# Latent attention's layer norms on ScalarE and GpSimd, its keys masked by GpSimd, and a beginning of one tile

## The chip, the cores and the metric

The kernel runs on one core of a Trainium2 chip. The metric is the device time of one execution in microseconds (us); less is better. Five engines work beside each other, each through its own queue of instructions in order: TensorE (PE, matmuls; its weight loads are PEld), VectorE (DVE), ScalarE (ACT), GpSimd (POOL) and SyncE (SP, which here only issues DMA transfers). SBUF is the memory that the engines work in, PSUM the one that matmuls write to.

## The reference

Four layers run over a tensor x of 32 x 256 tokens with 128 features, fp32. Each layer has an attention-like half and an MLP-like half, and each half works on a modulated layer norm:

```
mod = (silu(c) @ wmod).reshape(32, 6, 1, 128)       # sa, ca, ga, sb, cb, gb; gates held at 0.25 or more
h = layernorm(x) * (1 + ca) + sa;  x = x + ga * attn(h)
h = layernorm(x) * (1 + cb) + sb;  x = x + gb * ffn(h)
```

Layer 3's attention is the latent attention: 16 heads of 8 features, no mask, keys and values from a latent of 32 features.

```
q = h @ Wq + bq;  latent = h @ Wl + bl
k = latent @ Wk + bk;  v = latent @ Wv + bv
out = softmax(q k^T / sqrt(8)) v, per sequence of 256 tokens and per head;  out @ Wo + bo
```

Its MLP quantizes its input and weights to a 4-bit grid in blocks of 16 (fp4) before three matmuls with a SiLU gate. Layer 0's first half is a selective scan.

## The kernel before, in words

The 8192 tokens are 16 tiles (NB) of 512 tokens (TB), each kept in SBUF as x[b], 128 features by 512 tokens. The program goes through eight stages, two per layer: scan_layer, dense_moe, hale, capacity_moe, phase_attention, head_moe, latent_attention, fp4_mlp.

**Order.** A stage writes its work into an agenda of numbered slots (put(t, ...)) and then issues it slot by slot. mm (L386) and tr (L390), all matmuls and transposes, are always kept in that written order; VectorE's instructions too while `nc.vector.on` (L298 is the wrapper through which they go, so that most of VectorE's rows carry L298); ScalarE's only while `strict_act` is set, which it is in scan_layer and fp4_mlp and not in latent_attention. Where nothing is kept, a scheduler places the instruction in its engine's queue. The queue that results is fixed, and an engine that waits holds up all behind it.

**Beginning.** begin (L602 to L634) loads c and wmod of all four layers in one transfer, mw, computes the modulation of each layer (six matmuls, and copies into self.mods), and loads the 16 x tiles (xin; even ones through ScalarE's queue, odd ones through SP's), turns each by four transposes and copies it (by VectorE or ScalarE in turn) into x[b]. Only then the pools of scan_layer (L637) open. Its agenda begins at slot -44 of tile 0: norm_rows, scan_roots, norm_scale, norm_out and so on, a chain that reaches the first scan (hs, L849) at slot 0.

**Latent attention** (L2449). attention() gives a tile 16 slots, eight for each of two sequences. In each slot come first the score matmuls for the row maxima ("max", S<-kx,q; VectorE reduces them to mt), then those for the exponentials ("exp", S<-qa,kx; ScalarE writes E), then the rest: the values (po<-E,vz, two slots after their E), and the work on other tiles. Two sets of scores per slot share three PSUM buffers of S; one further buffer, tp, serves transposes and small matmuls, and one, po, the values. The queries qa carry the negated maximum in a ninth row of each head, taken in by a transpose of mt (tp<-cst,mt) at two slots per sequence.

The work before tile b is spread over the tile ahead of it: 14 slots ahead the norm's rows (head), 13 and 12 ahead its two parts, 10 ahead back (norm_out), 8 latent, 6 q, 4 keys, 2 v. Its output projection and residual come at slot 4 two tiles later, and from 3 slots after that the tile's MLP norm and quantization (mlp_front through mlp_ahead, tag fx and qx): mlp_norm at slot 7, its parts at 8 and 9, mlp_h at 11, mlp_rows at 15. The last tile's MLP norm lies in fp4_mlp. During tiles 7 to 9 the MLP's weights are quantized too.

**A norm** (two per tile): norm_rows (L440) turns x by four transposes into tp, ScalarE copies them to SBUF (ln_xn, or fx for the MLP), VectorE takes statistics (bn_stats, bn_aggr) and v = variance + eps (ln_v). norm_place (L456) then computes 1/sqrt(v) by an integer first guess and Newton steps on 128x4 values, all on VectorE (newton_parts, L934: 2 integer and 12 small operations in two parts), and scales the rows in place: four instructions of 128x128. norm_out turns the rows back (tp<-cst,ln_xn, or tp<-cst,fx).

**Keys** (keys, L1528): two matmuls put both halves of the 16 heads into S (128x1024). Four ScalarE activations (L1536) write kx: each 128x512 with a scale of one or zero per partition (c.half, which keeps one of two neighbouring heads) and a bias (key_bias, L133), which also writes the ones of the ninth row.

Of the kernel before, what the change touches and what calls it, by code (L numbers as in the profile page):

```python
# [25 lines left out]
ALU = mybir.AluOpType  # L26
# [115 lines left out]

def rows(v):

    v = np.asarray(v, np.float32).reshape(1, -1)
    return np.broadcast_to(v, (P, v.shape[1]))
# [29 lines left out]
def packs(d):  # L176
# [8 lines left out]
    k.add("cT", np.stack([np.asarray(d[f"L{n}_c"]).T for n in range(4)], 1))  # L185
    k.add("wmod", np.stack([np.asarray(d[f"L{n}_wmod"]) for n in range(4)], 1))
# [83 lines left out]
    k.add("Wk", spread(g["Wk"]))  # L270
# [3 lines left out]
    k.add("kb", key_bias(g["bk"]))  # L274
# [35 lines left out]
class Program:  # L310
# [162 lines left out]
    def norm_newton(self, mv, v, r):  # L473


        pool = self.nc.gpsimd
        t = self.wk("ln_t", (P, 4))
        pool.tensor_tensor(t, r, r, ALU.mult)
        pool.tensor_tensor(t, t, v, ALU.mult)
        pool.tensor_scalar(t, t, -0.5, 1.5, ALU.mult, ALU.add)  # L480
        pool.tensor_tensor(r, r, t, ALU.mult)
        shift = self.wk("ln_m", (P, 4))
        pool.tensor_tensor(shift, mv[:, :, 0], r, ALU.mult)
        pool.tensor_scalar(shift, shift, -1.0, None, ALU.mult)
        return r, shift

# [115 lines left out]
    def begin(self):  # L602
        nc, tc = self.nc, self.tc
        nc.scalar.preload_act_table_set(LN_EXP)
        with ExitStack() as ctx:
            self.pools(ctx, {"tp": 4, "mod": 2}, xin=3, mw=1)
            mw = self.wk("mw", (P, self.at["mod"]["n"]))
            nc.scalar.dma_start(mw, self.aps["mod"])
            v = View(mw, self.at["mod"]["at"])
            for n in range(4):  # L610
                sg = self.wk("sg", (P, NSEQ))
                self.sigmoid(sg, v.cT[:, n, :])
                nc.vector.tensor_tensor(sg, sg, v.cT[:, n, :], ALU.mult)
                ps = self.ps("mod", (P, 6, NSEQ))
                for j in range(6):
                    nc.tensor.matmul(ps[:, j, :], v.wmod[:, n, j * P : (j + 1) * P], sg, start=True, stop=True)
                m = self.mods[:, n]
                for j in (0, 3):
                    nc.scalar.copy(m[:, j, :], ps[:, j, :])
                    nc.vector.tensor_scalar(m[:, j + 1, :], ps[:, j + 1, :], 1.0, None, ALU.add)  # L620
                    neg, mag = self.wk("neg", (P, NSEQ)), self.wk("mag", (P, NSEQ))
                    nc.vector.tensor_scalar(neg, ps[:, j + 2, :], -1.0, None, ALU.mult)
                    nc.vector.tensor_tensor(mag, ps[:, j + 2, :], neg, ALU.max)
                    nc.vector.tensor_scalar(mag, mag, 0.25, 2.0, ALU.max, ALU.mult)
                    nc.vector.tensor_scalar(neg, ps[:, j + 2, :], 0.0, 0.5, ALU.is_ge, ALU.subtract)
                    nc.vector.tensor_tensor(m[:, j + 2, :], neg, mag, ALU.mult)
            xd = self.aps["x"].rearrange("(b t p) f -> b p t f", p=P, t=4)
            for b in range(NB):
                xi = self.wk("xin", (P, 4, P))
                (nc.sync if b % 2 else nc.scalar).dma_start(xi, xd[b])  # L630
                ps = self.ps("tp", (P, 4, P))
                for t in range(4):
                    nc.tensor.transpose(ps[:, t, :], xi[:, t, :], self.c.ident)
                (nc.scalar.copy if b % 2 else nc.vector.tensor_copy)(self.x[b], ps.rearrange("p a b -> p (a b)"))  # L634


    def scan_layer(self, w):  # L637
# [7 lines left out]
        with ExitStack() as ctx:  # L645
            self.pools(
                ctx, {"dB": 1, "hT": 1, "y": 1, "tp": 1},
                h=4, z=3, dl=3, duT=3, bc=3, xn=1, ln_xn=1, xp=1, y=1, yT=1, rows=1, Xc=1, du=1, sg=1, hsT0=1, hsT1=1, sp_m=1, sp_r=1, Xr=1,
# [21 lines left out]

            for p in range(-1, 8 * NB + 3):
                put(2 * p, self.scan_even, s, p)
                put(2 * p + 1, self.scan_odd, s, p)
# [854 lines left out]
    def keys(self, h, w, bias):  # L1528

        k4 = self.wk("kx", (P, 2, 2, TB))  # L1530
        pk = self.ps("S", (P, 2, TB))
        for x in (0, 1):
            self.mm(pk[:, x, :], w[:, x, :], h)
        for x in (0, 1):
            for j in (0, 1):
                self.nc.scalar.activation(  # L1536
                    k4[:, x, j, :],
                    pk[:, x, :],
                    AF.Identity,
                    bias=bias[:, x, j : j + 1],  # L1540
                    scale=self.c.half[:, j : j + 1],
                )
        return k4
# [905 lines left out]
    def latent_attention(self, w):  # L2449
        nc, c = self.nc, self.c  # L2450
        self.mlp_start()
        with ExitStack() as ctx:
# [7 lines left out]
            def before(b, tiles):  # L2460
                t = tiles[b] = {"vz": self.vzs[4 * (b % 2) : 4 * (b % 2) + 4]}

                def head():
                    t["st"] = self.norm_rows(self.x[b])
                    t["norm"] = self.norm_place(*t["st"])
# [17 lines left out]
                def k():  # L2483
                    t["k4"] = self.keys(t["lat"][:32, :], w.Wk, w.kb)
# [101 lines left out]
    def mlp_norm(self, a):  # L2586
        a["st"] = self.norm_rows(self.x[a["b"]], tag="fx")
        a["norm"] = self.norm_place(*a["st"])
# [211 lines left out]
```

## Time and profile before

| | us |
|---|---|
| three timed runs | 6774.54, 6795.66, 6796.21 (median 6795.66) |
| the profiled execution, whole | 6771.9 |
| its span in the profile | 6769.9 |
| beginning, until TensorE's first transposes for a norm | 44.8 |
| latent stage, tiles 2 to 14 (5784.4 to 6446.9) | 662.5 |
| last stage (6560 to 6770) | 210, VectorE 194 of it busy |

Granted clock of TensorE over the span: 0.918. How to read the lines that follow: a row of the profile names line, engine, operation and tile, output<-inputs, then the shape and count. Times are microseconds, and in rows of groups the mean is in nanoseconds. In brackets stands how long the engine was idle before it and which instruction ended that (<-). A row of a stretch gives from:to, length, and the busy time of each engine with its count of instructions. In rows of waits stand total, times and longest.

### The profile page before, as it was taken

Reading aid. Unit: us, or ns where it says so; the run is one execution under the profiler, and the core shown is the slowest. Engines: PE = TensorE matmul, PEld = TensorE weight load, DVE = VectorE, ACT = ScalarE, POOL = GpSimd, SP = SyncE. Lnnn points to the kernel's source line nnn. Section 1 sums busy time; section 2 is a strip of 40 time slices with the busy share of each in tenths; the row PEclk is TensorE's granted clock in tenths of the full one; section 3 lists DMA queues with packets and bytes.
Section 4 is the critical chain, followed back from the end, with each engine's and each line's share of the span. In section 5 each row is a group of like instructions: output and inputs, shape, how many; then the busy total and the mean of one; then the engine's idle time right before and its main releaser. Section 6 shows DMA issues by size and latency. Waiting matters only on the chain. (4 is left out here: it accounts for less than half of the span.)

```text
span 6769.9 us, 132928 instructions
## 1 busy us (share of the span) xinstructions
PE 5927.9 (88%) x54369; PEld 3341.0 (49%) x54369; DVE 4278.6 (63%) x9929; ACT 3493.9 (52%) x5035; POOL 2650.5 (39%) x2882
## 2 busy tenths in 40 slices
PE   5888886999899999999999767999889998999987
PEld 3555554466455555555566434555422222444444
DVE  3777776611455555555565644777777775677779
ACT  4888884333344444444444322443468886545542
POOL 3555553565444444444444443434234543000000
PEclk6999997999899999999999877888989998999998
DMA  1110111144000000000000101111134442000010
GB/s 60 41 41 29 41 41 35 42 124 119 15 6 5 5 8 5 5 8 5 5 2 2 47 17 26 26 24 26 31 79 90 92 91 49 16 18 18 18 33 30
DMA packets 175445, 232.19 MB, mean 34 GB/s; under 512 B 46519, under 2 KB 95919, under 8 KB 174450
## 3 DMA queue, kind: packets, MB, share of 16 engines
q1 hardware_dynamic: 120656, 124.40, 7.2%
q0 software_dynamic: 26992, 56.62, 3.5%
q10 hardware_dynamic: 27186, 42.67, 1.7%
q8 instruction: 426, 6.98, 0.4%
q14 instruction: 185, 1.52, 0.1%
HBM read 88.22 MB, written 74.97 MB: 24 GB/s over the span
## 5 line engine op out<-in xcount | busy, mean ns | idle before, releaser
L1418 ACT ACTIVATE E<-S 128x1024 f32<-128x1024 f32 x448 | 458.6, 1024 | 602.6 <-PE S L386 535.5
L298 DVE TENSOR_REDUCE mt<-S 128x4 f32<-128x1024 f32 (+1 forms) x512 | 549.8, 1087 | 252.5 <-PE S L386 196.1
L849 DVE TENSOR_TENSOR_SCAN hs<-decay,dB 128x512 f32<-128x512 f32 x512 | 583.0, 1204 | 91.8 <-PE dB L386 77.2
L386 PE MATMUL S<-qa,kx 32*128 32x256 f32 x4096 | 566.8, 396 | 59.8 <-DVE mt L298 39.0
L393 ACT ACTIVATE hid<-S,bigw 128x1024 f32<-128x1024 f32 x512 | 537.2, 1111 | 122.6 <-PE S L386 121.9
L1887 DVE TENSOR_TENSOR E<-S,cst 128x1024 f32<-128x1024 f32 x320 | 391.2, 1223 | 307.3 <-PE S L386 270.7
L1890 POOL TENSOR_SCALAR_AFFINE_SELECT E<-E 128x1024 f32<-128x1024 f32 x320 | 349.3, 1092 | 588.2 <-ACT E L1889 587.9
L386 PE MATMUL S<-kx,q 32*128 32x512 f32 (+1 forms) x2048 | 549.1, 631 | 16.9 <-ACT kx L1536 16.1
L1889 ACT COPY E<-S 128x1024 f32<-128x1024 f32 x320 | 323.5, 1011 | 328.4 <-PE S L386 244.7
L2439 POOL TENSOR_TENSOR acc<-acc,ye 128x512 f32<-128x512 f32 x256 | 344.5, 1346 | 362.7 <-DVE ye L298 319.6
L386 PEld LDWEIGHTS S<-qa,kx 32*128 32x128 f32 x4096 | 360.2, 200 | 178.4 <-DVE mt L298 107.1
L1719 DVE TENSOR_REDUCE mt<-S 128x4 f32<-128x512 f32 (+1 forms) x256 | 205.2, 823 | 320.9 <-PE S L386 312.4
L386 PE MATMUL S<-qG,f 32*128 32x512 f32 x2560 | 382.6, 658 | 4.5 <-DVE E L1887 3.4
L386 PE MATMUL S<-hm,bigw 32*128 32x512 f32 x2048 | 337.3, 650 | 24.8 <-ACT hid L393 24.8
L393 ACT ACTIVATE hsT<-hT 128x1024 f32<-128x1024 f32 x256 | 260.7, 1018 | 157.3 <-PE hT L390 156.2
L393 ACT ACTIVATE decay<-dl,A 128x510 f32<-128x510 f32 x512 | 339.1, 714 | 0.0
L386 PE MATMUL po<-E,vzl 128*32 128x128 f32 x8192 | 286.8, 281 | 59.6 <-POOL E L1890 59.3
L390 PE MATMUL hT<-cst,hs 128*128 128x128 f32 x2048 | 295.9, 290 | 22.6 <-ACT hsT L393 21.4
L386 PE MATMUL po<-hid,bigw 128*32 128x512 f32 x2048 | 279.9, 619 | 31.0 <-DVE ye L298 31.0
L386 PE MATMUL po<-E,vz 128*32 128x256 f32 x4096 | 304.7, 383 | 0.3 <-ACT oc L1438 0.2
L1422 POOL TENSOR_SCALAR_AFFINE_SELECT E<-E 128x512 f32<-128x512 f32 (+1 forms) x192 | 157.7, 822 | 364.4 <-ACT E L1418 363.9
L1766 ACT ACTIVATE E<-S 128x768 f32<-128x768 f32 (+1 forms) x192 | 168.9, 880 | 239.4 <-PE S L386 239.4
(524 smaller groups left out, 13192.1 us busy)
## 6 DMA issues: line engine op xcount, KB each, us to landing
gb<-gT SPq DMA_DIRECT2D x256, 256.0 KB
regions<-zeros ACTq DMA_DIRECT2D x16, 2048.0 KB
rx<-far SPq DMA_DIRECT2D x64, 256.0 KB
expert_rows<-eo SPq DMA_DIRECT2D x39, 256.0 KB
out<-out SPq DMA_DIRECT2D x16, 256.0 KB
xTd<-xT SPq DMA_DIRECT2D x15, 256.0 KB
xT<-xTd SPq DMA_DIRECT2D x15, 256.0 KB
bigw<-in_s SPq DMA_DIRECT2D x10, 256.0 KB
```

The lines of the kernel that those rows point to most:

```text
L298: return lambda *args, **kw: self.tc.keep_in_program_order(op(*args, **kw))
L386: return self.tc.keep_in_program_order(self.nc.tensor.matmul(out, lhsT, rhs, start=start, stop=stop, **kw))
L390: return self.tc.keep_in_program_order(self.nc.tensor.transpose(out, in_, self.c.ident[:k, :k]))
L393: ins = self.nc.scalar.activation(*args, **kw)
L849: nc.vector.tensor_tensor_scan(hs[:, :, n], decay, dB[:, :, n], 0.0, ALU.mult, ALU.add)
L1418: nc.scalar.activation(e, src, AF.Exp, scale=scale)
L1719: nc.vector.tensor_reduce(m.rearrange("p (g j) -> p g j", j=2), pm[:, :, x] if i == 0 else pm[:, :, :, 0:192], AX.X, ALU.max, negate=True,)
L1766: nc.scalar.activation(e, src, AF.Exp, scale=1.0 / math.sqrt(8))
L1887: nc.vector.tensor_tensor(e, src, self.c.caus.unsqueeze(1).to_broadcast([P, 8, P]), ALU.mult)
L1889: nc.scalar.copy(e, src)
L1890: nc.gpsimd.affine_select(e, e, [[0, 8], [1, P]], ALU.is_ge, 0.0, base=0, channel_multiplier=-1)
L2439: nc.gpsimd.tensor_tensor(a["acc"], a["acc"], ye, ALU.add)
```

## The change

Three edits. No work outside the beginning, latent attention and the MLP norms of fp4_mlp is edited.

1. *Beginning.* mod and x are brought in piece by piece. With the scan stage in the program, begin handles layer 0's modulation and x[0] alone; the other 15 tiles (load_in, turn_in) and three layers (mod_load, mod_layer) are put into scan_layer's agenda, at slots -45 to -15 (loads two slots before each turn) and -44 to -22. All x loads go through SP's queue, all x copies are VectorE's; loads of mod stay on ScalarE's queue.
2. *Norms of layer 3.* norm_apart takes norm_place's place: ln_v by GpSimd, Ln and Exp by ScalarE (norm_roots), one Newton step and the four scalings by GpSimd.
3. *Keys.* masked_keys: the bias is a 33rd row of the weights (key_row), against the row of ones that lat already has; one ScalarE copy of 128x1024 to SBUF (kk); two GpSimd multiplications by c.half, 128x1024 each, write kx.

```diff
--- before.py
+++ after.py
@@ -140,6 +140,13 @@
     return out.reshape(4, P).T.reshape(P, 2, 2)
 
 
+def key_row(b):
+
+    full = spread(np.asarray(b)[None]).reshape(1, 2, 8, 16)
+    full[:, :, :, 8] = 1.0
+    return full.reshape(1, 2, P)
+
+
 def rows(v):
 
     v = np.asarray(v, np.float32).reshape(1, -1)
@@ -182,8 +189,7 @@
         return g
 
     k = Pack()
-    k.add("cT", np.stack([np.asarray(d[f"L{n}_c"]).T for n in range(4)], 1))
-    k.add("wmod", np.stack([np.asarray(d[f"L{n}_wmod"]) for n in range(4)], 1))
+    k.add("mod", np.stack([np.concatenate([np.asarray(d[f"L{n}_c"]).T, np.asarray(d[f"L{n}_wmod"])], 1) for n in range(4)], 1))
     out["mod"] = k
 
     g, k = layer(0, "attn"), Pack()
@@ -267,11 +273,10 @@
     g, k = layer(3, "attn"), Pack()
     k.add("Wq", spread(g["Wq"]))
     k.add("Wl", g["Wl"])
-    k.add("Wk", spread(g["Wk"]))
+    k.add("Wk", np.concatenate([spread(g["Wk"]), key_row(g["bk"])], 0))
     k.add("Wo", gathered(g["Wo"]))
     k.add("Wv", np.concatenate([g["Wv"], g["bv"][None]], 0))
     k.add("bq", spread(g["bq"][None])[0].T)
-    k.add("kb", key_bias(g["bk"]))
     k.add("bo", col(g["bo"]))
     k.add("bl", g["bl"][:, None])
     out["s6"] = k
@@ -470,7 +475,7 @@
         self.act(r, t, AF.Exp, scale=-0.5)
         return r
 
-    def norm_newton(self, mv, v, r):
+    def norm_newton(self, mv, v, r, shifted=True):
 
 
         pool = self.nc.gpsimd
@@ -479,10 +484,23 @@
         pool.tensor_tensor(t, t, v, ALU.mult)
         pool.tensor_scalar(t, t, -0.5, 1.5, ALU.mult, ALU.add)
         pool.tensor_tensor(r, r, t, ALU.mult)
+        if not shifted:
+            return r, None
         shift = self.wk("ln_m", (P, 4))
         pool.tensor_tensor(shift, mv[:, :, 0], r, ALU.mult)
         pool.tensor_scalar(shift, shift, -1.0, None, ALU.mult)
         return r, shift
+
+    def norm_apart(self, xn, mv, v):
+
+        r = self.norm_roots(v)
+        yield
+        r, _ = self.norm_newton(mv, v, r, False)
+        for n in range(4):
+            self.nc.gpsimd.tensor_scalar(
+                xn[:, n, :], xn[:, n, :], mv[:, n, 0:1], r[:, n : n + 1], ALU.subtract, ALU.mult
+            )
+        yield
 
     def norm_scale(self, xn, r, shift):
         for n in range(4):
@@ -600,38 +618,51 @@
 
 
     def begin(self):
-        nc, tc = self.nc, self.tc
-        nc.scalar.preload_act_table_set(LN_EXP)
+
+        self.nc.scalar.preload_act_table_set(LN_EXP)
+        some = 0 in self.stages
         with ExitStack() as ctx:
-            self.pools(ctx, {"tp": 4, "mod": 2}, xin=3, mw=1)
-            mw = self.wk("mw", (P, self.at["mod"]["n"]))
-            nc.scalar.dma_start(mw, self.aps["mod"])
-            v = View(mw, self.at["mod"]["at"])
-            for n in range(4):
-                sg = self.wk("sg", (P, NSEQ))
-                self.sigmoid(sg, v.cT[:, n, :])
-                nc.vector.tensor_tensor(sg, sg, v.cT[:, n, :], ALU.mult)
-                ps = self.ps("mod", (P, 6, NSEQ))
-                for j in range(6):
-                    nc.tensor.matmul(ps[:, j, :], v.wmod[:, n, j * P : (j + 1) * P], sg, start=True, stop=True)
-                m = self.mods[:, n]
-                for j in (0, 3):
-                    nc.scalar.copy(m[:, j, :], ps[:, j, :])
-                    nc.vector.tensor_scalar(m[:, j + 1, :], ps[:, j + 1, :], 1.0, None, ALU.add)
-                    neg, mag = self.wk("neg", (P, NSEQ)), self.wk("mag", (P, NSEQ))
-                    nc.vector.tensor_scalar(neg, ps[:, j + 2, :], -1.0, None, ALU.mult)
-                    nc.vector.tensor_tensor(mag, ps[:, j + 2, :], neg, ALU.max)
-                    nc.vector.tensor_scalar(mag, mag, 0.25, 2.0, ALU.max, ALU.mult)
-                    nc.vector.tensor_scalar(neg, ps[:, j + 2, :], 0.0, 0.5, ALU.is_ge, ALU.subtract)
-                    nc.vector.tensor_tensor(m[:, j + 2, :], neg, mag, ALU.mult)
-            xd = self.aps["x"].rearrange("(b t p) f -> b p t f", p=P, t=4)
-            for b in range(NB):
-                xi = self.wk("xin", (P, 4, P))
-                (nc.sync if b % 2 else nc.scalar).dma_start(xi, xd[b])
-                ps = self.ps("tp", (P, 4, P))
-                for t in range(4):
-                    nc.tensor.transpose(ps[:, t, :], xi[:, t, :], self.c.ident)
-                (nc.scalar.copy if b % 2 else nc.vector.tensor_copy)(self.x[b], ps.rearrange("p a b -> p (a b)"))
+            self.pools(ctx, {"tp": 4, "mod": 2}, xin=3, mw=2)
+            for n in (0,) if some else range(4):
+                self.mod_layer(n, self.mod_load(n), self.ps("mod", (P, 6, NSEQ)))
+            for b in (0,) if some else range(NB):
+                self.turn_in(b, self.load_in(b), self.ps("tp", (P, 4, P)))
+
+    def mod_load(self, n):
+
+        mw = self.wk("mw", (P, NSEQ + 6 * P))
+        self.nc.scalar.dma_start(mw, self.aps["mod"][:, n * (NSEQ + 6 * P) : (n + 1) * (NSEQ + 6 * P)])
+        return mw
+
+    def mod_layer(self, n, mw, ps):
+
+        nc = self.nc
+        sg = self.wk("msg", (P, NSEQ))
+        self.sigmoid(sg, mw[:, :NSEQ])
+        nc.vector.tensor_tensor(sg, sg, mw[:, :NSEQ], ALU.mult)
+        for j in range(6):
+            self.mm(ps[:, j, :], mw[:, NSEQ + j * P : NSEQ + (j + 1) * P], sg)
+        m = self.mods[:, n]
+        for j in (0, 3):
+            nc.scalar.copy(m[:, j, :], ps[:, j, :])
+            nc.vector.tensor_scalar(m[:, j + 1, :], ps[:, j + 1, :], 1.0, None, ALU.add)
+            neg, mag = self.wk("neg", (P, NSEQ)), self.wk("mag", (P, NSEQ))
+            nc.vector.tensor_scalar(neg, ps[:, j + 2, :], -1.0, None, ALU.mult)
+            nc.vector.tensor_tensor(mag, ps[:, j + 2, :], neg, ALU.max)
+            nc.vector.tensor_scalar(mag, mag, 0.25, 2.0, ALU.max, ALU.mult)
+            nc.vector.tensor_scalar(neg, ps[:, j + 2, :], 0.0, 0.5, ALU.is_ge, ALU.subtract)
+            nc.vector.tensor_tensor(m[:, j + 2, :], neg, mag, ALU.mult)
+
+    def load_in(self, b):
+        xi = self.wk("xin", (P, 4, P))
+        self.nc.sync.dma_start(xi, self.aps["x"].rearrange("(b t p) f -> b p t f", p=P, t=4)[b])
+        return xi
+
+    def turn_in(self, b, xi, ps):
+
+        for t in range(4):
+            self.tr(ps[:, t, :], xi[:, t, :])
+        self.nc.vector.tensor_copy(self.x[b], ps.rearrange("p a b -> p (a b)"))
 
 
     def scan_layer(self, w):
@@ -645,7 +676,7 @@
         with ExitStack() as ctx:
             self.pools(
                 ctx, {"dB": 1, "hT": 1, "y": 1, "tp": 1},
-                h=4, z=3, dl=3, duT=3, bc=3, xn=1, ln_xn=1, xp=1, y=1, yT=1, rows=1, Xc=1, du=1, sg=1, hsT0=1, hsT1=1, sp_m=1, sp_r=1, Xr=1,
+                h=4, z=3, dl=3, duT=3, bc=3, xn=1, ln_xn=1, xp=1, y=1, yT=1, rows=1, Xc=1, du=1, sg=1, hsT0=1, hsT1=1, sp_m=1, sp_r=1, Xr=1, mw=1,
             )
             self.strict = self.strict_act = True
             wk = self.wk
@@ -668,6 +699,13 @@
             def put(t, f, *args):
                 agenda.setdefault(t, []).append((f, args))
 
+
+            for b in range(1, NB):
+                put(2 * b - 47, lambda b=b: s.update({("xi", b): self.load_in(b)}))
+                put(2 * b - 45, lambda b=b: self.turn_in(b, s["xi", b], self.ps("dB", (P, 4, P))))
+            for n in (1, 2, 3):
+                put(8 * n - 52, lambda n=n: s.update({("mw", n): self.mod_load(n)}))
+                put(8 * n - 46, lambda n=n: self.mod_layer(n, s["mw", n], self.ps("y", (P, 6, NSEQ))))
             for p in range(-1, 8 * NB + 3):
                 put(2 * p, self.scan_even, s, p)
                 put(2 * p + 1, self.scan_odd, s, p)
@@ -1542,6 +1580,23 @@
                 )
         return k4
 
+    def masked_keys(self, lat, w):
+
+        pk = self.ps("S", (P, 2, TB))
+        for x in (0, 1):
+            self.mm(pk[:, x, :], w[:, x, :], lat)
+        both = self.wk("kk", (P, 2, TB))
+        self.nc.scalar.copy(both, pk)
+        k4 = self.wk("kx", (P, 2, 2, TB))
+        for x in (0, 1):
+            self.nc.gpsimd.tensor_tensor(
+                k4[:, x],
+                both[:, x, :].unsqueeze(1).to_broadcast([P, 2, TB]),
+                self.c.half.unsqueeze(2).to_broadcast([P, 2, TB]),
+                ALU.mult,
+            )
+        return k4
+
 
     def hale(self, w):
         nc, c = self.nc, self.c
@@ -2461,8 +2516,8 @@
                 t = tiles[b] = {"vz": self.vzs[4 * (b % 2) : 4 * (b % 2) + 4]}
 
                 def head():
-                    t["st"] = self.norm_rows(self.x[b])
-                    t["norm"] = self.norm_place(*t["st"])
+                    t["st"] = self.norm_rows(self.x[b], nc.gpsimd)
+                    t["norm"] = self.norm_apart(*t["st"])
 
                 def part():
                     next(t["norm"])
@@ -2481,7 +2536,7 @@
                     t["q"] = self.query(t["h"], w.Wq, w.bq)
 
                 def k():
-                    t["k4"] = self.keys(t["lat"][:32, :], w.Wk, w.kb)
+                    t["k4"] = self.masked_keys(t["lat"], w.Wk)
 
                 def v():
                     pv = ps("tp", (P, 4, P))
@@ -2584,8 +2639,8 @@
         yield
 
     def mlp_norm(self, a):
-        a["st"] = self.norm_rows(self.x[a["b"]], tag="fx")
-        a["norm"] = self.norm_place(*a["st"])
+        a["st"] = self.norm_rows(self.x[a["b"]], self.nc.gpsimd, "fx")
+        a["norm"] = self.norm_apart(*a["st"])
 
     def mlp_h(self, a):
         a["h"] = self.norm_out(a["st"][0], self.ada_mods(3, 1, a["b"]), "fh")
```

## Prediction

> **What bounds the kernel now.** I read the page, then the busy times by stretch, TensorE's waits and the order of time in one tile. Busy columns are us of PE, PEld, DVE, ACT, POOL; then granted clock, DMA share, GB/s. The rows are tiles 2 to 14 of the latent stage, and tile 4 alone:
>
> ```profile
> PE 5927.9 (88%) x54369; PEld 3341.0 (49%) x54369; DVE 4278.6 (63%) x9929; ACT 3493.9 (52%) x5035; POOL 2650.5 (39%) x2882
> ...
> 5784.40:6446.90 662.50, 613.81 (x4879) 311.91 (x4879) 495.19 (x1247) 341.60 (x433) 5.68 (x11) 0.94 0.06 17
> 5883.50:5931.60 48.10, 44.61 (x376) 22.73 (x374) 37.35 (x95) 26.11 (x34) 0.52 (x1) 1.00 0.06 19
> ```
>
> TensorE bounds the stage: 44.61 of 48.10 us busy in tile 4, GpSimd idle. An average tile takes 662.5/13 = 50.96 us, 2.86 more than tile 4, at clock 0.94 instead of 1.00. What TensorE waits for in the 13 tiles (us in total, times, longest):
>
> ```profile
> PE S L386 <- DVE mt L298: 30.8, 37, 1.4
> PE S L386 <- ACT kx L1536: 14.0, 13, 1.1
> ```
>
> The two long waits of tile 4, in order of time (start, duration):
>
> ```profile
> 5897.33 0.88 DVE L298 SCALAR_TENSOR_TENSOR x<-y,mods,x 128x256 f32<-128x256 f32 x2 [1.26 <-ACT y L2504]
> ...
> 5899.30 1.11 DVE L298 TENSOR_SCALAR ln_xn<-ln_xn,ln_mv,ln_rs 128x128 f32<-128x128 f32 x4
> 5900.33 1.22 DVE L298 TENSOR_REDUCE mt<-S 128x4 f32<-128x1024 f32 x1
> 5901.61 1.13 PE L386 MATMUL S<-qa,kx 32*128 32x256 f32 x8 [1.40 <-DVE mt L298]
> ...
> 5921.60 2.78 ACT L1536 ACTIVATE kx<-S,w,cst 128x512 f32<-128x512 f32 x4 [0.91 <-PE S L386]
> ...
> 5924.44 0.70 PE L386 MATMUL S<-kx,q 32*128 32x512 f32 x2 [1.07 <-ACT kx L1536]
> ```
>
> The norm's second half (5898.13 to 5900.33) stands in VectorE's queue ahead of a maximum, and TensorE loses 1.40 us; four key copies hold a PSUM buffer of S, and it loses 1.07. Each happens once in every one of the 13 tiles. The other gaps of tile 4 (0.51, 0.41) follow fp4 work.
>
> The clock costs as much. In the 13 tiles 14 stretches at half clock last 81.6 us; 12 begin within 3.4 us of a gap of 1.20 to 1.40 us, one or two after a key gap.
>
> At the beginning, TensorE turns sixteen x tiles until 43 us and only then starts the chain that leads to the first scan at 127.52:
>
> ```profile
> 13.34 2.58 PE L633 MATMUL tp<-cst,xin 128*128 128x128 f32 x11 [13.34 <-DMA xin<-in_x]
> 44.80 1.11 PE L390 MATMUL tp<-cst,x 128*128 128x128 f32 x4 [0.36 <-ACT wd L658]
> 127.52 1.22 DVE L849 TENSOR_TENSOR_SCAN hs<-decay,dB 128x512 f32<-128x512 f32 x1 [5.00 <-ACT ln_xn L393]
> ```
>
> **What the Trainium skill says.** "TensorE: Matmul & The Clock Gate", Part 1: the clock is full or half and is judged over windows of about 3.4 us. The trace has only 1.0 and 0.5, in pieces of 3.41 us; but here halving follows pieces in which TensorE was busy 0.59 to 0.69, not idle ones, and the trace decides. "GPSIMD Engine Reference", sections 1 and 3.1: GpSimd can't read PSUM, takes about twice VectorE's time on two-input work, and shares its SBUF interface with it. The trace: 1.28 to 1.35 us against 0.69 at 128x512; of sharing below. "ScalarE: Activation LUTs", on table loads: about 1.28 us, and a drain as long; the trace shows 1.28 and the next activation at once.
>
> **Part 1, norms (two per tile).** VectorE loses 16 small operations (0.16 each, 0.196 apart) and four scalings (1.11): 3.1 + 1.1 = 4.2 us per norm. In the 1.40 us gap, 2.2 us of it leave the queue; the maximum can start when the residual ends (5898.2), ends at 5899.5, and TensorE wants it at 5900.20. The gap goes: 13 x 1.40 = 18.2 us. Next late there is nothing by 0.7 us.
>
> GpSimd gets, per norm, five 128x4 operations (0.20 to 0.23 us, 0.28 apart) and four scalings of 128x128. The latter aren't in the trace; nearest is uu, 128x512 with one scalar, 1.76 us. A quarter is 0.44; with overhead, bounds 0.44 and 0.9, taken 0.7 as a middle value. So 1.4 + 2.8 = 4.2 us.
>
> A wait is added on ScalarE: Ln waits for GpSimd's ln_v, and the changed order has Ln and Exp straight behind the copy of the rows, ahead of the E of that slot and of xT or lat. In tile 4 ln_v would be there at 5892.4, and Ln and Exp (0.2 each) end at 5893.0; E, now at 5891.78, slips 1.2 us, xT (5892.70) to 5894.1, so that the tp buffer comes free some 0.2 us after TensorE's 5894.59. E itself is used two slots later. The MLP's norm does the same at 5907.9: E 1.3 us late, lat done at 5910.5 before TensorE's 5910.86. Cost 0 to 0.5 per tile, taken 0.2: 15 x 0.2 = +3. GpSimd's rows are then ready near 5897 and 5912.7 against uses at 5903.24 and 5916.58: hidden by 4 us or more; the cover ends at a scaling of 1.6 us.
>
> The last tile's MLP norm falls where ScalarE has the Silu table: three table loads, 3 x 1.28 + 0.4 = 4.3 us, beside VectorE's 4.2 saved, where VectorE is the bound (194 of 210 us busy in the last stage). Bounds -4 and +4; taken -3, since sl, 6668.2 next, isn't needed before 6674.
>
> **Part 2, keys.** Four activations (2.78) become one copy of 128x1024 (1.01, the page's copy E<-S) with the bias as a 33rd row in the matmul, same count. S is free 1.7 us earlier, and the wait was 1.07: 13 x 1.07 = 14.0 us. GpSimd masks two halves; nearest row:
>
> ```profile
> L1841 POOL TENSOR_TENSOR qG<-f,cst 128x1024 f32<-128x1024 f32 x32 | 60.5, 1891 | 17.8 <-DVE f L1668 17.8
> ```
>
> 2 x 1.9 (up to 2.7): from 5922.6 to 5926.4 or 5928.1; first use near 5931. Hidden by 3 us. GpSimd's memset of lat, at 5927.39 until now, falls in behind the masks, and the next ln_v behind it; it is wanted at 5892 of a tile, 8 us later. Only the first tile waits for it: +2, with bounds 0 and +4.
>
> **Part 3, clock.** With 1.40 and 1.07 gone, the rest (0.5) leave TensorE 0.85 busy in a window, above any that was halved. I take 12 of 14 stretches as gone: 81.6 x 12/14 / 2 = 35 us; bounds 0 and 41. Three gaps of 1.10 in the weight tiles may keep some.
>
> Tile 1, outside the window, has one key gap and 10.1 us at half clock: -1.07 - 5.05 = -6.1.
>
> **Part 4, beginning.** Only layer 0's modulation (400 KB, was 1600) and one x are left ahead of the chain; weights no longer landing at 9.46 but near 6, x 0 is turned by about 10 to 13, and the chain starts near 14 instead of 44.80: -31. The other 15 x (all on SP now, behind two buffers) and three modulation layers stand in the chain's slots, in TensorE's written order: each x costs 0.6 to 1.1 us of PE and 0.69 of DVE, each layer 1.6 us. If all stood on the path: 15 x 1.1 + 3 x 1.6 = 21; some falls into waits (a norm takes 8.8 us, of which PE works 2.2), but SP's loads and the activations of the sigmoid ahead of ln_t add some. Taken 15 back: -16; bounds -28 and +5 (a late load blocks TensorE's order). The modulation loads go out from ScalarE's queue and have one buffer; each is issued two slots after the layer before it has freed that buffer, so I cost their wait at nothing; if the cover fails, ScalarE's next step of the chain waits for it, about 2 us each time.
>
> **Sum.** -18.2 - 14.0 - 35 - 6.1 + 3 + 2 - 3 - 16 = -87 against the profiled execution's 6771.9 us (span 6769.9). The three runs are 6774.5, 6795.7, 6796.2, so the profile lies 24 below their median. I subtract from the mean of all four, 6784.6: 6697 us.
>
> **Rivals.** *A, the clock stays.* The half-clock stretches come back behind other gaps or by their own period: for it, tile 1 had one without a long norm gap; against it, undisturbed tiles have no gap less. -87 + 35 + 5 = -47: 6738. *B, the beginning gives nothing:* turn-ins and loads take all 31 us; for it, TensorE runs in a written order; against, most of the chain is latency. -71: 6714. *C, more:* all stretches and the best beginning, -87 - 6 - 12 = -105: 6680. *D, slower, by the shared interface:* GpSimd now works about 13 us per tile beside VectorE. Overlapped VectorE rows elsewhere: oT 0.68 and 0.68, vz 0.28 and 0.37, the residual 0.39 and 0.91: factors 1.0 to 2.4. VectorE would be busy (38.1 - 8.4)/45.5 = 65%, so 8.5 us per tile are exposed; at factor f it loses 8.5 (f - 1), at worst all ahead of maxima. To cancel 87 us over 15 tiles takes 5.8 per tile: from f = 1.7 the change is slower. At f = 2: 15 x 8.5 = +128, 6825. Against it: maxima read PSUM, and oT, with two SBUF inputs, didn't slow.
>
> **Chances.** Likeliest 0.50, its own range 6680 to 6720; A 0.20, B 0.15, C 0.09, D 0.06. Range 6660 to 6750: it takes in A and B, and C's far bound, without D. 0.3% of 6795.7, about 20 us, is what a measurement can tell: below 6775 lie all but D, and a D of small factor (0.05 to 0.06 near no change). Faster 0.91, same 0.05, slower 0.04.
>
> **What would show it.** The waits for mt by 1.40 and for kx by 1.07 are gone; tiles take 45.5 to 46 us (44.6 busy, 0.9 gaps); the granted clock of tiles 2 to 14 is over 0.98; the first scan comes at 105 to 117 us; the two halves of kx end before the next tile's first S. Wrong would be: mt durations above 1.22, waits for ln_xn, fx or kx out of POOL, or half-clock stretches as long as before.

## The result, and the profile after

The changed kernel takes 6690.5 us (median of four runs, 6667.6 to 6696.0) against 6794.9 (6774.5 to 6796.2): ratio 0.9847, 95% interval 0.9831 to 0.9863, that is 93 to 115 us less. The prediction was 6697 us (6660 to 6750): 87 us less than the mean of 6784.6 that it started from, 99 less than the median of the runs known then. Later a second chip gave 6594.2 against 6694.8, ratio 0.9849 (0.9832 to 0.9867). The chips differ by about 100 us in the kernel before, so kernels are compared below only with runs of their own chip, as ratios.

The same views of the changed kernel as of the kernel before: the page, and the stretches of tiles 2 to 14 and of one tile without half clock (columns PE, PEld, DVE, ACT, POOL busy, then granted clock, DMA share, GB/s).

```profile
PE 5879.2 (88%) x54369; PEld 3325.6 (50%) x54369; DVE 4184.3 (63%) x9329; ACT 3471.9 (52%) x5045; POOL 2849.2 (43%) x3202
```

```profile
5781.40:6364.00 582.60, 569.32 (x4885) 293.98 (x4883) 410.66 (x754) 324.89 (x446) 162.31 (x271) 1.00 0.06 20
5869.90:5914.60 44.70, 43.71 (x376) 22.52 (x374) 30.95 (x57) 24.87 (x35) 12.56 (x21) 1.00 0.06 20
```

The 13 tiles went from 662.5 to 582.6 us and the clock in them from 0.94 to 1.00; the undisturbed tile from 48.1 to 44.7. VectorE's 95 instructions in a tile became 57, and GpSimd is busy for 12.56 of 44.70 us instead of 0.52. TensorE's busy time in a tile fell too, from 44.61 to 43.71, with the same 376 matmuls; this is the part that the prediction didn't have. TensorE's waits in the 13 tiles (us in total, times, longest):

```profile
PE S L391 <- DVE mt L303: 9.2, 22, 0.5
PE tp L395 <- DVE qx_xn L303: 3.3, 3, 1.1
```

The 1.40 us waits for mt and the 1.07 us waits for kx are gone, and no wait for GpSimd or for E has come. In time (start, duration), the changed tile where the 1.40 us gap was, and GpSimd's and ScalarE's new work:

```profile
5878.76 0.23 POOL L458 TENSOR_SCALAR ln_v<-ln_mv 128x4 f32<-128x4 f32 x1 [12.56 <-DVE ln_mv L303]
5880.70 3.13 POOL L500 TENSOR_SCALAR ln_xn<-ln_xn,ln_mv,ln_rs 128x128 f32<-128x128 f32 x4
5906.20 3.74 POOL L1592 TENSOR_TENSOR kx<-kk,cst 128x1024 f32<-128x1024 f32 x2 [9.01 <-ACT kk L1589]
```

```profile
5879.02 0.21 ACT L398 ACTIVATE ln_t<-ln_v 128x4 f32<-128x4 f32 x1 [2.87 <-POOL ln_v L458]
5879.26 0.21 ACT L398 ACTIVATE ln_rs<-ln_t 128x4 f32<-128x4 f32 x1
5879.37 1.00 ACT L1456 ACTIVATE E<-S 128x1024 f32<-128x1024 f32 x1
```

```profile
5885.41 0.70 PE L391 MATMUL S<-kx,q 32*128 32x512 f32 x2
5885.85 0.48 PE L391 MATMUL S<-qa,kx 32*128 32x256 f32 x2
5885.94 0.59 PE L391 MATMUL S<-kx,q 32*128 32x512 f32 x2
5886.17 0.81 PE L391 MATMUL S<-qa,kx 32*128 32x256 f32 x6
```

Ln did wait 2.87 us for ln_v with E queued behind it, as forecast, and nobody waited for that E. GpSimd's rows are ready at 5883.8 and wanted at 5887.5, its kx at 5909.9 and wanted at 5914.3. The last fence is the point. In the kernel before, one set of scores ran alone:

```profile
5899.08 1.13 PE L386 MATMUL S<-kx,q 32*128 32x512 f32 x4
```

Then came 1.40 us of nothing, then S<-qa,kx alone (1.13). Now the second set starts inside the first and both are done in 1.57 us.

The beginning, the first scan:

```profile
111.25 1.22 DVE L887 TENSOR_TENSOR_SCAN hs<-decay,dB 128x512 f32<-128x512 f32 x1 [5.00 <-PE dB L391]
```

16.3 us earlier than 127.52; 16 was forecast. Changed minus before in these two profiles, in us: end of the scan -16.7, the latent stage's first transposes for a norm +0.1, its first scores +2.8, start of tile 2 -3.0, end of tile 14 -82.9, end of the program -82.1. The profiled executions thus show 22 us less gain than the medians, and the beginning's lead used up before the latent stage. The beginning alone, below, settles that. The 2.7 us between the stage's first transposes and its first scores are the change's own. There nothing covers GpSimd's work, and TensorE waits 2.70 us for its kx, where it waited 0.45 for ScalarE's:

```profile
5703.18 3.92 PE L391 MATMUL S<-kx,q 32*128 32x512 f32 x12 [2.70 <-POOL kx L1592]
```

### The profile page after: what moved, and what is told of

Read it like the earlier page. It is cut to its first block, busy times and chain, and to the rows that moved or that the text cites. A ratio compares the mean times of both kernels' runs of the same rounds, so it can differ in the third digit from the quotient of the medians.

```text
span 6687.8 us, 132577 instructions
## 1 busy us (share of the span) xinstructions
PE 5879.2 (88%) x54369; PEld 3325.6 (50%) x54369; DVE 4184.3 (63%) x9329; ACT 3471.9 (52%) x5045; POOL 2849.2 (43%) x3202
## 5 line engine op out<-in xcount | busy, mean ns | idle before, releaser
L391 PE MATMUL S<-qa,kx 32*128 32x256 f32 x4096 | 538.9, 386 | 37.1 <-issue 20.4
L391 PEld LDWEIGHTS S<-qa,kx 32*128 32x128 f32 x4096 | 346.7, 195 | 131.0 <-DVE mt L303 65.4
```

The costliest lines, as they stand in the source:

```text
L391: return self.tc.keep_in_program_order(self.nc.tensor.matmul(out, lhsT, rhs, start=start, stop=stop, **kw))
```

## The experiments

All ratios are to the kernel before on the same chip, with 95% intervals.

| kernel | ratio | us against before |
|---|---|---|
| beginning alone | 0.9975 (0.9965 to 0.9986) | -17 |
| keys alone | 0.9987 (0.9979 to 0.9996) | -9 |
| norms alone | 0.9883 (0.9860 to 0.9905) | -79 |
| changed, VectorE held 5 additions | 0.9928 (0.9910 to 0.9945) | -49 |
| changed kernel again | 0.9849 (0.9832 to 0.9867) | -101 |
| changed, VectorE held 3 additions | 0.9867 (0.9849 to 0.9884) | -89 |
| changed, keys' bias on ScalarE | 0.9831 (0.9816 to 0.9845) | -113 |
| changed, norm of phase attention too | 0.9844 (0.9828 to 0.9860) | -104 |
| changed, scalings three times as long | 1.0057 (1.0039 to 1.0076) | +38 |
| both improvements | 0.9815 (0.9802 to 0.9829) | -124 |
| both, first tile as before | 0.9808 (0.9789 to 0.9826) | -131 |

**The beginning alone.** The kernel before, with begin, mod_load, mod_layer, load_in, turn_in and their slots from the change.

> The kernel before with the new beginning alone. Theory: the first scan comes 16 us earlier (111 instead of 127.5 us), the rest of the program keeps its order, and all 16 us reach the end: -16 us. Rival 1: a later stage waits for something that the beginning doesn't move (in the two profiles the lead of 16.7 us at the end of the scan stage is gone by 4150 us): 0, within 5 us, and the lead vanishes at the same place as in the changed kernel. Rival 2: the lead vanishes in the profile at another place or not at all, and comes through in the medians: then what took it there was an accident of one execution.

-17 us, interval -24 to -9, and the first scan at 109.8. In its profile the lead over the two kernels of the same chip that keep the old beginning is 18 to 20 us at the end of the scan, 28 to 37 at the first keys of the phase attention, and not used up anywhere. Rival 1 is out. What took the lead in the first profile of the changed kernel came in stages whose instructions the change doesn't touch and whose length differs from execution to execution. Over the profiles of before, of the changed kernel and of the first four experiments, hale took 2107.5 to 2121.1 us from the first to the last instruction of its own lines (before 2114.7, changed 2120.0), and the way from there to the phase attention 333 to 354 (before 333, the shortest of the six; changed 342.5). So rival 2 holds: an accident of single executions.

**The keys alone.**

> The kernel before with the new keys alone (copy, GpSimd masks, bias in the matmul). Theory: the 13 waits of 1.07 us for kx and the one of tile 1 go (-15), and with them only the half-clock stretches that follow a key gap, two or three of 15 (-10): -25 us; about 70 us at half clock stay in tiles 2 to 14. Rival, the clock follows no gaps: -15. Rival, GpSimd's masks are late: waits for kx out of POOL take their place, 0.

```diff
-                    t["k4"] = self.keys(t["lat"][:32, :], w.Wk, w.kb)
+                    t["k4"] = self.masked_keys(t["lat"], w.Wk)
```

-9 us, interval -14 to -3: a third of what was expected, and less than the gaps alone. Its 13 tiles and a tile without half clock:

```profile
5795.00:6436.80 641.80, 606.44 (x4885) 303.40 (x4883) 493.64 (x1247) 319.82 (x394) 54.35 (x37) 0.97 0.06 18
5889.50:5937.10 47.60, 45.19 (x376) 22.68 (x374) 37.25 (x95) 24.45 (x31) 4.26 (x3) 1.00 0.06 19
```

The gap for kx is gone, but the tile lost 0.5 us (48.1 to 47.6), not 1.07: TensorE is busy 45.19 instead of 44.61. A later run below says why. In this one execution the 13 tiles are at half clock for 44.4 us where about 70 were expected, and 20.7 us shorter than in the profile of before. The medians of 22 runs don't show so much, so whether the keys' gaps bore on the clock stays open here.

**The norms alone.**

> The kernel before with the new norms alone. Theory: the 13 waits of 1.40 us and the three of 1.2 to 1.3 in the weight tiles go (-22), and with them the half-clock stretches that followed them, all but some 15 us of 81.6 (-33); with -3 for the last stage: -58 us, and waits of 1.07 for kx stay. Rival, the clock follows no gaps: half clock in tiles 2 to 14 stays near 80 us and the gain is -25. Rival, keys and norms each leave a gap that is enough to halve the clock: e2 and e3 together fall short of the changed kernel by 20 us or more.

```diff
-                    t["st"] = self.norm_rows(self.x[b])
-                    t["norm"] = self.norm_place(*t["st"])
+                    t["st"] = self.norm_rows(self.x[b], nc.gpsimd)
+                    t["norm"] = self.norm_apart(*t["st"])
```

-79 us, interval -95 to -64: more than expected. Its 13 tiles and one of them, and its waits:

```profile
5800.00:6392.00 592.00, 564.79 (x4885) 296.24 (x4883) 411.63 (x753) 346.60 (x485) 114.03 (x245) 0.99 0.06 20
5891.00:5936.20 45.20, 43.13 (x376) 22.57 (x374) 31.06 (x58) 26.55 (x38) 8.85 (x19) 1.00 0.06 20
```

```profile
PE S L386 <- ACT kx L1549: 14.0, 13, 1.1
PE S L386 <- DVE mt L298: 9.2, 22, 0.5
```

Thirteen gaps of 1.07 are still there, yet the clock is 0.99 (two stretches, 6.8 us, each behind such a gap). A tile is 2.9 us shorter than before: 1.40 of gap, and 1.5 of busy time (44.61 to 43.13) in which nothing was taken off TensorE. Slot by slot, 0.69 of the busy time went in the slot of the gap, and 0.68 in the two slots in which VectorE did the MLP norm's small operations. There the kernel before shows no gap at all. A maximum stood behind eight small operations, and the second set of scores, which begins 0.06 us after that maximum's end, came late into the first:

```profile
5910.55 1.22 DVE L298 TENSOR_REDUCE mt<-S 128x4 f32<-128x1024 f32 x1
5911.23 1.13 PE L386 MATMUL S<-kx,q 32*128 32x512 f32 x4
5911.83 1.13 PE L386 MATMUL S<-qa,kx 32*128 32x256 f32 x8
```

The scores of that maximum were through at 5909.9. With the norms alone the maximum starts 0.05 us after its scores, and the second set, again 0.05 behind its end, 0.25 after the first instead of 0.60:

```profile
5915.23 1.23 DVE L298 TENSOR_REDUCE mt<-S 128x4 f32<-128x1024 f32 x1 [1.02 <-PE S L386]
5916.26 0.70 PE L386 MATMUL S<-kx,q 32*128 32x512 f32 x2
5916.51 0.48 PE L386 MATMUL S<-qa,kx 32*128 32x256 f32 x2
```

The last stage is 3.2 us shorter, near the 3 forecast for the last MLP norm.

**The gap put back without the norm.**

```diff
+            self.bufs["pad"] = 1
+            pad = wk("pad", (P, 256))
...
+                def hold():
+                    part()
+                    for n in range(5):
+                        nc.vector.tensor_tensor(pad, self.x[b][:, 0:256], self.x[b][:, 0:256], ALU.add)
...
-                return [(-13, part, "last"), (-12, part, "last")] + [(*work, "late") for work in works]
+                return [(-13, part, "last"), (-12, hold, "last")] + [(*work, "late") for work in works]
```

> The changed kernel with VectorE held up again where the norm's second part was: five additions of 128x256 (x + x into a scratch tile that nothing reads), about 2 us, in each attention norm; the norm itself stays on ScalarE and GpSimd. It puts back the gap and nothing else. In the changed kernel the maximum there ends 0.7 us before TensorE is through with its other scores, so the gap is 1.3 us. Theory, a gap of 1.2 us or more halves the clock: +17 us of gaps and about 11 or 12 half-clock stretches in tiles 2 to 14 (70 us, cost 35): +50 us against the changed kernel, 6740. Rival, the clock recovered for another reason (less work on VectorE, or the time of day of the chip): +17 alone, half clock near 0.

Its 13 tiles, one of them, and the waits:

```profile
5782.80:6412.30 629.50, 598.88 (x4885) 304.10 (x4883) 434.92 (x818) 325.16 (x446) 162.31 (x271) 0.96 0.06 19
5878.30:5925.00 46.70, 44.35 (x376) 22.53 (x374) 32.75 (x62) 24.82 (x35) 12.57 (x21) 1.00 0.06 19
```

```profile
PE S L391 <- DVE mt L303: 26.9, 35, 1.4
```

Ratio 0.9928 where the changed kernel has 0.985: about +54 us, 50 expected. Nine stretches of half clock (47.8 us, where 70 were expected) came back, each within 3 us of a gap of 1.36; the changed kernel has none. VectorE is busy for 32.75 us in a tile, far less than the 37.35 of before, so it isn't the amount of its work that takes the clock down. The rival falls. The tile without half clock is 2.0 us longer than 44.7: 1.36 of gap and 0.64 of busy time. So a late maximum by itself also makes TensorE longer busy; over 13 tiles that is 8 us, which makes up for most of the half clock that stayed away.

**A smaller hold.** The same with three additions.

> As the kernel that holds VectorE up by five additions, with three: about 1.2 us, of which 0.7 are free, so a gap of 0.5 in each tile. Theory, a gap takes the clock down only if it leaves a window of 3.4 us too empty, and 0.5 us never did: no half clock in tiles 2 to 14, and 13 x 0.5 to 1.2 us = +6 to +16 against the changed kernel (with the overlap of the two sets of scores that is lost beside the gap). Rival, any late maximum does it in proportion: 25 to 30 us at half clock.

```profile
5686.70:6283.90 597.20, 578.11 (x4885) 293.91 (x4883) 423.76 (x792) 325.11 (x446) 162.93 (x271) 1.00 0.06 20
5777.50:5823.30 45.80, 44.36 (x376) 22.52 (x374) 31.93 (x61) 24.86 (x35) 12.61 (x21) 1.00 0.06 19
```

No half clock; +9.9 us in the medians of the same chip, +14.6 in the 13 tiles, inside the 6 to 16. The gap is 0.45 us and the tile 1.1 longer: again 0.65 of busy time besides. At 0.45 and at 1.36 the loss is the same: in both the second set starts only after the first has ended.

**Which gaps take the clock down.** Counted over the profiles of before and of the first four experiments, in tiles 2 to 14: of 61 gaps of 1.20 to 1.40 us, 39 were followed by a half-clock stretch; of 39 gaps of 1.07 for kx, 6; of 15 of 1.1 for qx_xn and of 93 near 0.5, none. The Trainium skill ("TensorE: Matmul & The Clock Gate", Part 1) has windows of 3.4 us that run free. The traces agree: within each profile all half-clock stretches begin on one grid of 3.413 us, from the first stage to the last. Laid on that grid, the gaps of 1.20 to 1.40 part: of 29 that fall whole into one window, all were followed by half clock; of 32 that lie across two, 10. By TensorE's busy share of a window at full clock, in these five profiles: under 0.64, 33 of 33 were followed by half clock; from 0.64 to 0.70, 12 of 53; above, none of 777. A gap of 1.07 alone leaves 0.69, one of 0.5 leaves 0.85. The bound is one of these tiles: with GpSimd three times as long, three windows between 0.60 and 0.64 were not followed by half clock, and in dense_moe, in the profile of before, 7 of 7 windows of 0.77 to 0.80 were.

**The 33rd row.** The prediction took the keys' matmul at the same cost with the bias in it. The changed kernel, with 32 rows and the bias on ScalarE (the packing of the weights and the new argument are left out here):

```diff
-        self.nc.scalar.copy(both, pk)
+        for x in (0, 1):
+            self.nc.scalar.activation(both[:, x, :], pk[:, x, :], AF.Identity, bias=bias[:, x : x + 1])
...
-                    t["k4"] = self.masked_keys(t["lat"], w.Wk)
+                    t["k4"] = self.masked_keys(t["lat"][:32, :], w.Wk, w.kb)
```

> The changed kernel with the keys' bias taken out of the matmul: 32 rows as before, and two ScalarE activations of 128x512 with a bias (1.26 us, as q has) in place of one copy (1.01). In the profiles a tile free of half clock loses its 1.07 us gap for kx but becomes only 0.5 us shorter, TensorE being 0.6 us longer busy, and slot 12, where the keys' matmuls are, takes 3.77 us in each kernel with the 33rd row and 2.75 in each without it. Theory, 33 rows keep TensorE from working on scores in the other rows meanwhile: slot 12 goes back to 2.75 or so, a tile takes 43.7 us, and the whole is 13 to 16 us shorter than the changed kernel. Rival, slot 12 is longer because the work around it moved: 44.7 us per tile and no change, or +2 by the longer activations.

The keys' matmuls (S<-lat,w) and the scores behind them, first in the changed kernel, then in this one:

```profile
5903.09 1.98 PE L391 MATMUL S<-lat,w 33*128 33x512 f32 x4
5905.00 0.70 PE L391 MATMUL S<-kx,q 32*128 32x512 f32 x2
```

```profile
5799.98 1.12 PE L392 MATMUL S<-lat,w 32*128 32x512 f32 x2
5800.58 0.70 PE L392 MATMUL S<-kx,q 32*128 32x512 f32 x2
5800.94 0.59 PE L392 MATMUL S<-lat,w 32*128 32x512 f32 x1
5800.95 0.48 PE L392 MATMUL S<-qa,kx 32*128 32x256 f32 x1
```

With 33 rows the keys run alone for 1.9 us; with 32 the scores enter between them after 0.6. The three slots from the keys' matmuls on (each from its first S<-kx,q to the next slot's) went from 8.95 to 8.30 us, a tile from 44.7 to 44.05. The skill's page (Part 3, on packing) says that matmuls whose tiles lie in different row groups run at the same time; the trace agrees for 32 rows, and shows what one row more takes away. 6577.9 us (6573.9 to 6584.4) against 6594.2 (6584.6 to 6594.6) of the changed kernel on that chip: 16 less, as in the two profiles, which place 8.4 in tiles 2 to 14, 3.6 in the latent stage ahead of them and 1.4 behind. The other 2.6 lie ahead of the stage, where the edit changes nothing. So some 13 are the edit's, the lower end of the 13 to 16. The rival falls, though the theory's 43.7 for a tile was too good by 0.35.

**The changed kernel again**, beside these.

> The changed kernel again, beside the next three on the same chip. The three parts measured alone gave -17, -9 and -79 against the kernel before; if they only add up, -105: ratio 0.9845. Its profile should show the beginning's lead of 16 to 18 us kept to the latent stage, which the first profile of it didn't, if what took it there was an accident; tiles 2 to 14 at 582 to 584 us without half clock.

0.9849: the three parts add up (-17, -9, -79: -105 of some 6790). Tiles 2 to 14 took 582.6 us, to the tenth as on the first chip. Whether the lead is kept can't be read from this profile, as there is none of the kernel before on its chip; the beginning alone has told it.

**GpSimd three times as long.** Two more instructions behind each scaling, which add zero:

```diff
+            for _ in range(2):
+                self.nc.gpsimd.tensor_scalar(
+                    xn[:, n, :], xn[:, n, :], self.zeros[:, 0:1], self.zeros[:, 1:2], ALU.add, ALU.add
+                )
```

> The changed kernel with GpSimd's scalings three times as long: after each scaling of 128x128 two more that add zero (same form, 0.79 us). Theory: the prediction's cover ends near 1.6 us per scaling. At 2.4 us the rows of the attention norm come 2.6 us after TensorE wants them (now ready at 5883.8, wanted at 5887.5; 6.3 us are added) and those of the MLP norm 3.4 us after: waits of 2.6 and 3.4 us out of GpSimd in every tile, TensorE's clock taken down by each, a tile of 52 to 56 us in place of 44.7: 110 to 170 us slower than the changed kernel, which is slower than the kernel before by 10 to 70. Rival, sharing of the SBUF interface: VectorE's maxima get longer than 1.22 us beside a GpSimd that now works 25 of 45 us. Rival, something else hides it: under +50.

```profile
PE tp L395 <- POOL fx L504: 29.5, 28, 3.6
PE tp L395 <- POOL ln_xn L504: 29.3, 26, 1.8
```

1.0057, +38 against before and about +138 against the changed kernel, as expected: the cover is there and ends. Of the waits, that for the attention norm's rows reached 1.8 us where 2.6 was forecast, that for the MLP norm's 3.6 where 3.4 was, and half clock came back (92 us between 5720 and 6440). So somewhere between 0.79 and 2.4 us per scaling the change turns slower than the kernel before. VectorE's maxima still take 1222 ns beside twice the GpSimd work, as 1220 in the changed kernel and 1222 before, oT 692 against 681: of the sharing of the interface, rival D, nothing that counts was met. Four scalings of 0.79 us, 3.13 per norm, are hidden; 9.4 are not.

**The same norm in the phase attention.**

> The changed kernel with the same norm (Ln and Exp on ScalarE, Newton step and scalings on GpSimd) in the phase attention too, whose 16 tiles still have VectorE's norm. There the norm's second part stands ahead of a maximum as well (a gap of 0.85 us in the tile from 4362 to 4410 us), and the stage is at half clock for 217 of 792 us. Theory, the gap and a part of the clock come back: -14 of gaps, -10 to -30 of clock: 20 to 40 us shorter than the changed kernel. Rival, that stage's other gaps (scores with a mask, 1.2 to 1.4 us) are enough to keep the clock down: -5 to -14. Rival, GpSimd, which masks E there (284 of 789 us busy), gets E late: slower by up to 10.

-9.6 us in the medians of that chip, with intervals that overlap. In the profile the stage from its first keys took 714.7 us against 743.1, with 83.8 us at half clock against 136.9: the theory's size. But the first keys came 54.2 us after the stage's start instead of 34.5:

```profile
4102.05 0.22 POOL L483 TENSOR_TENSOR ln_t<-ln_rs 128x4 f32<-128x4 f32 x1
4102.43 1.02 POOL L1280 DMA_INDIRECT got<-eo,back  x1 [0.16 <-issue]
4103.48 0.21 POOL L484 TENSOR_TENSOR ln_t<-ln_t,ln_v 128x4 f32<-128x4 f32 x1
```

Each small operation of the first norm stands behind an indirect gather that GpSimd issues for the residual rows. None of the expectations had this wait. The late E that the rival named is small: TensorE's waits for masked E went from 6.9 to 11.3 us over the stage.

**Both improvements**, and then both with tile 0 of the phase attention left to VectorE:

> Both improvements on the changed kernel: the keys' bias on ScalarE with 32 rows (measured -16 on the changed kernel), and the norm of the phase attention on ScalarE and GpSimd (-10 in the medians, -28 in the stage of the profile). Theory: they add up, ratio 0.980 to 0.982 to the kernel before, against 0.985 of the changed kernel; phase attention at 26 to 30 us less than in the changed kernel's profile on the same chip class. Rival: the phase attention's gain is lost again in another stage, ratio 0.983 as with the bias alone.

```diff
-                    t["st"] = self.norm_rows(self.x[b], nc.gpsimd)
-                    t["norm"] = self.norm_apart(*t["st"])
+                    t["st"] = self.norm_rows(self.x[b], nc.gpsimd if b else None)
+                    t["norm"] = (self.norm_apart if b else self.norm_place)(*t["st"])
```

> Both improvements, but the first tile of the phase attention keeps VectorE's norm. In the profiles with that norm on GpSimd the stage's first keys come 54.2 us after its start instead of 34.5: ln_v and each of the Newton steps stand behind indirect gathers of 1.0 to 1.3 us in GpSimd's queue. Theory: that prologue goes back to about 34.5 us, the stage keeps its 28 us, so 18 to 20 us less than both improvements as they were: ratio to the kernel before near 0.979. Rival: the gathers of later tiles hold up the later norms too and the prologue was only the first of them: ratio 0.9815 as before.

0.9815 and 0.9808: both beat the changed kernel's 0.985; the step from one to the other is inside the intervals. In the profile the last one has its first keys after 34.5 us again, and its stage took 758.1 us where six profiles of kernels on a chip of its speed took 789 to 793. So the place of the 20 us is shown; that the whole is 18 to 20 us shorter is not. One of the five runs came to 6642.5 and the others to 6661 to 6667.

## Why the prediction was right, and where its steps were off

**Norms: right in mechanism, mis-sized.** The sum's term was the gap, 13 x 1.40 = 18.2 us. In tiles without half clock the norms alone gave 2.9 us per tile, 38 us over 13. The missing half is busy time of TensorE: 44.61 to 43.13 us, with the same matmuls. A maximum that comes late keeps the second set of scores from running beside the first. For the slot of the gap (0.69 of the 1.5) the two holds show it apart from the norm: a gap of 0.45 or of 1.36 costs 0.65 us more in busy time each. For the MLP norm's two slots (0.68) the traces show the order of events, but no run put that delay back alone. The prediction looked for what ends in a wait, and took 44.6 as a floor; so it expected tiles of 45.5 to 46, and they take 44.7. Here the skill ("Perfetto Trace Analysis", on identifying the most-contended engine) warns that a matmul row's busy time is a poor measure because matmuls are pipelined; this case agrees: 93% busy hid 3% that could be removed. GpSimd's scaling took 0.79 us where 0.7 was taken from bounds of 0.44 and 0.9, within the cover.

**The added wait: over-priced.** ScalarE stood 2.9 us before Ln, and E came 1.2 us after its scores, as forecast; but no wait of TensorE for E, tp or lat is in the 13 tiles. +3 was taken, bounds 0 to 0.5 per tile; it was the lower bound.

**Keys: the gap went, the gain didn't.** 14.0 was forecast; with the norms already done the keys gave 0.5 us per tile (45.2 to 44.7). The step that failed is "with the bias as a 33rd row in the matmul, same count": same count of instructions, not the same company for them. GpSimd's mask took 1.89 us, as its nearest row.

**Clock: right, with two errors that cancel.** 12 of 14 stretches were taken as gone, at half their length each: 35 us. All went, 81.6 us at half clock to none in both profiles of the changed kernel, so rival A fell. But tiles of the kernel before that hold such a stretch are 0.36 to 0.46 us longer per us of it, not 0.5 (tile 5: 3.7 for 10.2; tile 11: 2.8 for 6.8), since other waits hide in it. 81.6 x 0.4 = 33. That the gap behind a late maximum was the cause, which the prediction had only from sequence in time, is shown by the hold of five additions.

**Beginning: right.** -16 forecast, 16.3 in the first scan, 17 (9 to 24) in the whole, so rival B fell. The chain began at 14.82, 30.0 us earlier (31 forecast), and the turn-ins took 13.7 back (15 taken).

**Small terms.** From the stage's first scores to tile 2, tiles 0 and 1 gave 5.8 us; -6.1 was forecast for tile 1. The +2 for the first tile's wait met +2.7 ahead of its first scores: 1.6 by the masks, which were meant, and 1.1 by the first norm, whose scalings nothing covers there, a path that the prediction put at nothing. The last stage, from its first table load on, is 0.9 us shorter in the changed kernel's profile and 1.1 to 1.2 in its repetition, both holds and the kernel with the bias on ScalarE (-3 forecast), and 3.2 with the norms alone; why the two differ isn't shown. The three table loads came as forecast, 1.28 us each.

**The sum.** The norms gave some 20 us more than their term and the keys 7 less. From the latent stage's first transposes to the end the two profiles show 82 us, where the terms without the beginning make 71. With the 17 of the beginning alone that is 99, inside the 93 to 115 of the medians. The number 6697 came nearer to 6690.5 than 87 came to 104, because its base of 6784.6 lay 10 us under the median of 6794.9. That part is luck.

## What to carry to other kernels

A wait in a profile may cost more than its length, and a late result may cost without any wait: here matmuls of 32 rows ran beside one another only if the second set was ready in time, and that loss stands in the busy row, so compare busy times of equal work before calling one a floor. Before moving small work to an idle engine, look at that engine's queue at each place where the work will land, the prologue too; and before folding a bias into a matmul as one more row, ask what else ran in the rows that it now takes.

## What wasn't expected of the hardware

- Gaps of 1.2 to 1.4 us in a TensorE that is else over 90% busy took its clock to one half for 3.4 or 6.8 us in 39 of 61 cases, gaps of 1.07 for kx in 6 of 39; what decided was whether the gap fell whole into one window of a fixed grid of 3.413 us (29 of 29) or across two (10 of 32).
- Four matmuls of 33 rows ran 1.98 us alone where four of 32 rows, with scores of other rows among them, let the scores start after 0.6.
- On GpSimd a scaling of 128x128 with two scalars per partition took 794 ns, 0.78 apart, where VectorE takes 342.
